# Mamba blocks of a four-layer megakernel: X for one pair of images, deeper rings with sums one group later, output projection and fusion in one accumulation, statistics by ScalarE, and the last sum of softplus moved

## The chip, the cores and the metric

The kernel runs on one core of one Trainium2 chip, in float32 throughout. The metric is the device time of one launch in microseconds (us). Before the change it is 9826.69 us, the median of 3 runs (9817.78 to 9828.18).

## The reference, cut to what matters

Four layers follow one another on an image tensor x of 4 x 96 x 64 x 64. Layers 0 and 2 are the Mamba block below (the only code that the change touches); layer 1 is another state-space block and layer 3 a ConvNeXt block. In layers 0 and 2:

```python
# seq: (b, L=4096, 96), two sublayers i; DIN=192, DSTATE=16, DTRANK=6
seq = seq + _mamba_block(seq, ...)          # for i in range(2)
#   h = layernorm(seq); xs, z = split(h @ in_w)
#   xc = silu(causal 4-tap conv of xs)
#   dt, Bm, Cm = split(xc @ xproj_w)
#   delta = softplus(dt @ dt_w + dt_b);  dA = exp(delta * A)
#   hstates = scan over L of  s = dA * s + delta * Bm * xc
#   y = (hstates . Cm + Dp * xc) * silu(z);  return y @ out_w
gp = relu(x.mean((2, 3)) @ gp_w.T + gp_b)   # global branch, from the input
out = fus_w @ concat([mamba_out, gp broadcast]) + fus_b
out = (out - mean(out)) * rsqrt(var(out) + EPS) * bn_g + bn_b   # over batch and pixels
return out + residual
```

## The kernel before, in words

The four images go in two pairs. One step of `Scan.run` (L383) is one pair, one sublayer (`sub`) and one chunk of T = 512 positions, so a Mamba stage has 2 x 2 x 8 = 32 steps, and the launch has two such stages. Channels of both images of a pair (2 x 192) fill three 128-row tiles j.

**Front.** `mamba_front` (L155) makes what a step needs: layernorm (PE, ScalarE, VectorE, GpSimd), convolution and projections on PE into the two PSUM banks "mm", SiLU, then delta by `softplus` (L260) and `du = delta * xz`. The 128 x 512 tiles delta and du go to DRAM (`dd`, `dg`, L251), from where the scan reads them with a broadcast over the 16 states. It is a generator: the scan loop takes one or two pieces of the next step's front per group (`PACE`, L256), so front and scan of neighbouring steps run together.

**Groups.** A step has 24 groups (j, q, half), each two scans of 128 x 512. Group n passes these stages at these lags (L395 on): `load` (L288, lag -4: SyncE, called SP, issues the broadcast DMAs into a ring "da" of 6 tiles), `decay` and `spread` (-2 and -1: ScalarE takes exp of delta times A; PE spreads du into the PSUM ring "bs", L313, or, in one group of four, du arrives by DMA and GpSimd multiplies it by B, L308), `scan` (0: VectorE multiplies by B, L335, and runs two scans into `hs`, L340; GpSimd multiplies by C into `hc`, L342), `sums` (+2: PE sums hc over the states into `py`, L361). `hs` and `hc` have 3 buffers each. After the last group of a j, `close` (+3, L369) multiplies py by silu(z) on VectorE, `project` (+4, L377) is the output projection on PE into `po`, with VectorE adding it to X (L381), and `fuse` (+5, sublayer 1 only) multiplies X by the fusion weights (L510), adds the bias on ScalarE (L511), takes `bn_stats` on VectorE (L512) and stores the chunk (L513). [...]The order within a queue follows the program only roughly: the tile framework's scheduler moves single instructions past one another, so lines that neighbour in the code need not neighbour in the trace.

**X.** The residual stream of all four images stays in SBUF, 4 x 4096 floats in each of 96 partitions. It is loaded once (L473, L525), and VectorE sums each image over its 4096 positions (L532) for the global branch.

Of the kernel before, what the change touches and what calls it, by code (L numbers as in the profile page):

```python
# [18 lines left out]
F32 = mybir.dt.float32  # L19
AF = mybir.ActivationFunctionType  # L20
# [134 lines left out]
def mamba_front(tc, k, X, pools, wt, pair, c, h, made):  # L155
# [14 lines left out]
    for b in range(2):  # L170
        pc = bank("pc")[:C]
        nc.tensor.matmul(
            pc, lhsT=k.center, rhs=X[:, 2 * pair + b, ds(c * T, T)], start=True, stop=True
        )
        sq = work.tile([P, T], F32, tag="ua", name="sq")[:C]
        nc.scalar.activation(sq, pc, AF.Square)
        yield
        pv = bank("pv")[:C]
        nc.tensor.matmul(pv, lhsT=k.mean, rhs=sq, start=True, stop=True)
        rs = work.tile([P, T], F32, tag="lg", name="rs")[:C]  # L180
        rsqrt(k.act, rs, pv, k.eps[:C])
        yield
        dst = h[:C, b, 3 : 3 + T]
        nc.vector.tensor_tensor(dst, pc, rs, ALU.mult)
        nc.gpsimd.tensor_scalar(dst, dst, wt["ln"][:, 0:1], wt["ln"][:, 1:2], ALU.mult, ALU.add)
# [45 lines left out]
    for j in range(3):  # L231
        pt = bank("pt")
        for r0, r1, d0, d1, b in SEGS[j]:
            half = ds(HALFP * b, HALFP)
            nc.tensor.matmul(
                pt[r0:r1], lhsT=wt["dt"][half, d0:d1], rhs=dbl[half], start=True, stop=True,
            )
        delta = work.tile([P, T], F32, name="delta", bufs=2)
        softplus(nc, k.act, work, delta, pt)
        yield  # L240
        if j == 0:
            for b in range(2):
                for q in range(2):
                    r = HALFP * b + (QUART if q else RANK + 1)
                    nc.sync.dma_start(
                        bc[:, b, q], rows[r : r + NST, None].to_broadcast([NST, HEIGHT, T])
                    )
        nc.gpsimd.tensor_tensor(du[:, j], delta, xz[:, j], ALU.mult)
        for name, x in (("dd", delta), ("dg", du[:, j])):
            made[name, j] = dram.tile([P, T], F32, name=f"{name}{j}")  # L250
            nc.sync.dma_start(made[name, j], x)  # L251
# [8 lines left out]
def softplus(nc, act, work, out, x):  # L260

    u = work.tile([P, T], F32, tag="ua", name="ua")
    t = work.tile([P, T], F32, tag="lg", name="lg")
    nc.scalar.activation(u, x, AF.Abs)
# [5 lines left out]
    nc.vector.scalar_tensor_tensor(t, x, 1.0, u, ALU.subtract, ALU.subtract, reverse1=True)  # L270
    nc.gpsimd.tensor_tensor(out, out, t, ALU.add)


class Scan:
# [8 lines left out]

    def __init__(self, tc, k, X, pools, sel, carry, fuse):
        self.tc, self.k, self.X, self.sel, self.carry, self.fuse = tc, k, X, sel, carry, fuse
        self.state, self.psum = pools

    def load(self, g):  # L288

        for name, which in (("da", "dd"), ("du", "dg")) if g["dma"] else (("da", "dd"),):  # L290
            g[name] = self.state.tile([P, GS, T], F32, tag="da", name=name, bufs=6)
            for i in range(GS):
# [37 lines left out]
    def scan(self, g):  # L330
# [3 lines left out]
        if not g["dma"]:  # L334
            nc.vector.tensor_tensor(dbx, dbx, self.b_or_c(g, 0), ALU.mult)  # L335
        hs = self.state.tile([P, GS, T], F32, name="hs", bufs=3)
        for i in range(GS):
            n = NQU * g["quarters"][i] + g["q"]
            init = 0.0 if c == 0 else self.carry[:, j, n : n + 1]
            nc.vector.tensor_tensor_scan(hs[:, i], da[:, i], dbx[:, i], init, ALU.mult, ALU.add)  # L340
        g["hc"] = self.state.tile([P, GS, T], F32, name="hc", bufs=3)
        nc.gpsimd.tensor_tensor(g["hc"], hs, self.b_or_c(g, 1), ALU.mult)  # L342
# [28 lines left out]
    def project(self, g, b):  # L371

        nc = self.tc.nc
        xz, wt = g["made"]["xz"], g["wt"]
        po = self.psum.tile([P, T], F32, tag="po", name="po", bufs=1)[:C]
        for n, (j, r0, r1) in enumerate(ROWS[b]):
            nc.tensor.matmul(  # L377
                po, lhsT=wt["out"][r0:r1, j], rhs=xz[r0:r1, j], start=(n == 0), stop=(n == 1)
            )
        xs = self.X[:, 2 * g["pair"] + b, ds(g["c"] * T, T)]  # L380
        nc.vector.tensor_tensor(xs, xs, po, ALU.add)  # L381

    def run(self, steps, wts, front, first):  # L383
# [12 lines left out]
        ahead = iter(())  # L396
        for n in range(-4, total + 6):
            slot = (n + LEAD) % each
# [8 lines left out]

            if (g := at(3)) and g["last"]:
                self.close(g)
            for stage, lag in (  # L410
                (self.load, -4), (self.spread, -1), (self.decay, -2), (self.scan, 0), (self.sums, 2),
            ):
                if g := at(lag):
                    stage(g)

            for lag, what in ((4, self.project), (5, self.fuse)):
                if (g := at(lag)) and g["last"] and g["j"] and (g["sub"] or lag == 4):
                    what(g, g["j"] - 1)
# [48 lines left out]
def mamba_fusion(ctx: ExitStack, tc, k, src, dst, w):  # L467

    nc = tc.nc
    one = ctx.enter_context(tc.tile_pool(name="m1", bufs=1))  # L470
    X = one.tile([C, B, L], F32, name="X")
    for b in range(2):
# [27 lines left out]
    for q in range(NQU):  # L500
        pq = psum.tile([P, T], F32, tag="mm", name="pq")[:, :QUART]
        nc.tensor.transpose(pq, sel["du"][:QUART, 0, q], k.ident[:QUART, :QUART])
        nc.vector.tensor_copy(sel["sum"][:, q], pq)
    stats = one.tile([C, B * NT, nc.vector.BN_STATS_DIM], F32, name="stats")

    def fuse(g, b):
        b, c = 2 * g["pair"] + b, g["c"]
        xs = X[:, b, ds(c * T, T)]
        pf = psum.tile([P, T], F32, tag="po", name="pf", bufs=1)[:C]
        nc.tensor.matmul(pf, lhsT=fus[:, 0], rhs=xs, start=True, stop=True)  # L510
        nc.scalar.activation(xs, pf, AF.Identity, bias=gb[:, b : b + 1])  # L511
        nc.vector.bn_stats(stats[:, b * NT + c], xs)  # L512
        nc.sync.dma_start(dst[b, :, ds(c * T, T)], xs)  # L513

# [7 lines left out]

    for b in range(B):
        rest = slice(T if b < 2 else 0, L)
        nc.sync.dma_start(X[:, b, rest], src[b, :, rest])  # L525

    gsum = one.tile([C, B], F32, name="gsum")
    made = {}
    for n, _ in enumerate(front(0, made)):
        if n % 4 == 3 and n // 4 - 1 in range(B):  # L530
            b = n // 4 - 1
            nc.vector.reduce_sum(gsum[:, b : b + 1], X[:, b], axis=AX.X)  # L532
    wts.append(mamba_weights(nc, k.act, k.ident, one, w, 1, one7))

# [4 lines left out]
    vec = one.tile([C, 4], F32, name="vec")  # L539
    nc.sync.dma_start(vec, w["vecs"])  # L540


# [8 lines left out]

    Scan(tc, k, X, (state, psum), sel, carry, fuse).run(steps, wts, front, made)

    norm = k.norms.pop()
    mv = one.tile([C, 2], F32, name="mv")
    nc.vector.bn_aggr(mv, stats)
    sc, sh = norm[:, 0:1], norm[:, 1:2]
    rsqrt(k.act, sc, mv[:, 1:2], k.eps[:C])
    nc.vector.tensor_tensor(sc, sc, vec[:, 2:3], ALU.mult)
    nc.vector.tensor_tensor(sh, mv[:, 0:1], sc, ALU.mult)  # L560
    nc.vector.tensor_tensor(sh, vec[:, 3:4], sh, ALU.subtract)
# [848 lines left out]
```

## Time and profile before

| what | value |
|---|---|
| median of 3 runs | 9826.69 us |
| the profiled execution, its own time | 9824.4 us |
| its span (first to last instruction) | 9822.7 us |
| first Mamba stage (layer 0) | 0 to 3062 us |
| layer 1 | 3062 to about 6176 us |
| second Mamba stage (layer 2) | about 6176 to 9237 us |
| layer 3 | 9237 to 9822.7 us |
| mean granted TensorE clock over the span | 0.939 |

How it is read: a row of a group gives busy time and the mean of one instruction, and after the bar the idle time of the engine ahead of these instructions with what ended it ("<-"). A row by stretch gives, for a window of time, each engine's busy time and number of instructions, then the granted clock, the mean share of the 16 DMA engines and the bandwidth. PEld is weight loading, SPq the queue of SyncE that issues DMAs. Most questions are put to the window from 200 to 2900 us, in which steps of the first stage follow one another. It holds 88 instructions of L369, three to a step, so 29.33 steps of 92.05 us.

### The profile page before, as it was taken

How to read it: one execution, taken by the hardware profiler on the slowest of the kernel's cores; microseconds unless marked ns; L12 is line 12 of the kernel's file. 1: busy time of each engine (PE TensorE's matmuls, PEld its weight loads, DVE VectorE, ACT ScalarE, POOL GpSimd, SP SyncE). 2: the span in 40 equal slices, each digit the busy share in tenths (PEclk: the TensorE clock that was granted, in tenths of full speed). 3: DMA queues.
4: the chain of work that ended last, by engine and by line, in shares of the span. 5: the costliest groups of instructions: out<-in, count | busy, mean ns of one | idle time of the engine just before them, and what ended most of it. 6: DMA issues, size and time to landing. Idle time of an engine off the chain costs nothing. (4 is left out here: it accounts for less than half of the span.)

```text
span 9822.7 us, 110113 instructions
## 1 busy us (share of the span) xinstructions
PE 8432.2 (86%) x32750; PEld 3481.8 (35%) x32750; DVE 8131.3 (83%) x11036; ACT 5529.8 (56%) x10516; POOL 6879.9 (70%) x4573
## 2 busy tenths in 40 slices
PE   7888888888886998998998889788888888888678
PEld 1222212222222776776776767212212122222122
DVE  7999999999995666666666667699999999999787
ACT  5566566666663455555445555466666666666345
POOL 6888888888884555555555555588888888888511
PEclk8999999999997999999999999899999999999789
DMA  7677777777774222222222321576777777777653
GB/s 184 199 206 205 201 209 203 205 207 200 205 204 134 69 73 81 82 67 83 81 67 77 86 69 60 156 203 201 207 207 201 209 202 201 207 204 201 163 120 83
DMA packets 810274, 1528.80 MB, mean 156 GB/s; under 512 B 126381, under 2 KB 131913, under 8 KB 805834
## 3 DMA queue, kind: packets, MB, share of 16 engines
q1 hardware_dynamic: 809674, 1521.76, 55.1%
q8 instruction: 260, 4.26, 0.2%
q14 instruction: 340, 2.79, 0.1%
HBM read 1224.56 MB, written 150.08 MB: 140 GB/s over the span
## 5 line engine op out<-in xcount | busy, mean ns | idle before, releaser
L342 POOL TENSOR_TENSOR hc<-hs,bc 128x1024 f32<-128x1024 f32 x1536 | 3610.4, 2357 | 626.5 <-DVE hs L340 560.6
L340 DVE TENSOR_TENSOR_SCAN hs<-da,carry,bs 128x512 f32<-128x512 f32 x2016 | 2467.0, 1265 | 81.1 <-DVE bs L335 2.3
L107 ACT ACTIVATE da<-da,w_a 128x512 f32<-128x512 f32 x2304 | 1616.3, 716 | 1265.9 <-DMA da<-dd 1220.7
L361 PE MATMUL py<-hc,selsum 128*32 128x512 f32 x6144 | 1795.7, 636 | 466.4 <-POOL hc L342 453.2
L313 PE MATMUL bs<-du,seldu 64*128 64x512 f32 x4608 | 1572.6, 676 | 211.1 <-DVE hs L340 199.2
L335 DVE TENSOR_TENSOR bs<-bs,bc 128x1024 f32<-128x1024 f32 x1152 | 1398.3, 1214 | 181.6 <-PE bs L313 178.4
L308 POOL TENSOR_TENSOR du<-du,bc 128x1024 f32<-128x1024 f32 x384 | 905.5, 2358 | 272.5 <-DMA du<-dg 149.3
L361 PEld LDWEIGHTS py<-hc,selsum 128*32 128x32 f32 x6144 | 239.9, 110 | 1810.2 <-POOL hc L342 1124.8
L879 POOL TENSOR_TENSOR seg<-seg,cb 128x384 f32<-128x384 f32 x512 | 515.3, 1008 | 513.9 <-DVE cb L878 429.7
L313 PEld LDWEIGHTS bs<-du,seldu 64*128 64x128 f32 x4608 | 446.2, 195 | 1205.4 <-DVE hs L340 857.5
L863 DVE TENSOR_SCALAR seg<-dr,dac 128x128 f32<-128x128 f32 x1536 | 646.7, 455 | 271.5 <-PE y L908 264.2
L194 PE MATMUL pu<-h,w_conv 96*128 96x512 f32 (+3 forms) x2048 | 835.6, 628 | 8.8 <-ACT rs L107 8.7
L340 DVE TENSOR_TENSOR_SCAN hs<-bs,carry,du 128x512 f32<-128x512 f32 x672 | 823.6, 1260 | 7.5 <-issue 3.8
L814 PE MATMUL front<-pk,sconv 128*128 128x512 f32 x1536 | 756.4, 610 | 30.1 <-ACT z L802 24.8
L918 POOL TENSOR_TENSOR y<-y,xs 128x192 f32<-128x192 f32 x496 | 295.4, 595 | 626.2 <-DVE y L917 619.4
L931 ACT ACTIVATE y<-yz 128x192 f32<-128x192 f32 x512 | 186.1, 363 | 910.7 <-DVE yz L930 909.8
L883 POOL TENSOR_TENSOR xs<-pre,coef 128x576 f32<-128x576 f32 x512 | 598.8, 1174 | 64.6 <-ACT pre L112 32.3
L825 PE MATMUL front<-sconv,pk 128*128 128x192 f32 x3072 | 573.9, 330 | 51.5 <-DVE pre L830 46.2
L345 ACT COPY carry<-hs 128x2 f32<-128x2 f32 x1344 | 250.8, 187 | 571.0 <-DVE hs L340 567.3
L825 PEld LDWEIGHTS front<-sconv,pk 128*128 128x128 f32 x3072 | 497.5, 190 | 82.3 <-DVE pre L830 72.6
L107 ACT ACTIVATE bs<-da,w_a 128x512 f32<-128x512 f32 x768 | 522.0, 680 | 3.7 <-DMA da<-dd 1.5
L908 PEld LDWEIGHTS y<-xs,seg 128*128 128x128 f32 x3072 | 439.9, 205 | 142.4 <-issue 79.6
(200 smaller groups left out, 13612.7 us busy)
## 6 DMA issues: line engine op xcount, KB each, us to landing
da<-dd SPq DMA_DIRECT2D x3072, 256.0 KB
du<-dg SPq DMA_DIRECT2D x768, 256.0 KB
dr<-rows SPq DMA_DIRECT2D x256, 384.0 KB
bc<-rows SPq DMA_DIRECT2D x256, 256.0 KB
dd<-delta SPq DMA_DIRECT2D x192, 256.0 KB
dg<-du SPq DMA_DIRECT2D x192, 256.0 KB
pk<-xn SPq DMA_DIRECT2D x128, 384.0 KB
pk<-xn SPq DMA_DIRECT2D x128, 256.0 KB
```

The lines of the kernel that those rows point to most:

```text
L107: self.last = self.scalar.activation(out, in_, func, **kw)
L194: nc.tensor.matmul(pu[r0:r1], lhsT=wt["conv"][:kk, tap, d0:d1], rhs=h[:kk, b, ds(tap, T)], start=(tap == 0), stop=(tap == 3),)
L308: nc.gpsimd.tensor_tensor(g["du"], g["du"], self.b_or_c(g, 0), ALU.mult)
L313: nc.tensor.matmul(g["bs"][:, i], lhsT=self.sel["du"][rows, g["half"], g["q"]], rhs=g["made"]["du"][rows, g["j"]], start=True, stop=True,)
L335: nc.vector.tensor_tensor(dbx, dbx, self.b_or_c(g, 0), ALU.mult)
L340: nc.vector.tensor_tensor_scan(hs[:, i], da[:, i], dbx[:, i], init, ALU.mult, ALU.add)
L342: nc.gpsimd.tensor_tensor(g["hc"], hs, self.b_or_c(g, 1), ALU.mult)
L361: nc.tensor.matmul(py[rows], lhsT=self.sel["sum"][:, g["q"]], rhs=g["hc"][:, i], start=(g["q"] == 0), stop=(g["q"] == NQU - 1),)
L814: nc.tensor.matmul(p, lhsT=self.conv[:, i, DI + q * DST : DI + (q + 1) * DST], rhs=pk[:, i, ds(c * T, T)], start=(i == 0), stop=(i == 2),)
L825: nc.tensor.matmul(p, lhsT=pk[:, i, ds(c * Q, Q)], rhs=self.conv[:, i, :DI], start=(i == 0), stop=(i == 2),)
L863: nc.vector.tensor_scalar(seg[:, h], g["pair"]["dr"][:, c % 2 * NH + h], made["dac"][:, n0 + h : n0 + h + 1], 0.0, ALU.subtract, ALU.min,)
L883: nc.gpsimd.tensor_tensor(xs, x.to_broadcast([P, 3, NH, HD]), coef.to_broadcast([P, 3, NH, HD]), ALU.mult)
```

## The change

What it does: X holds one pair (the second pair's chunks are loaded over the first pair's as these are stored, and the sums of images 2 and 3 are taken from pieces that pass through the "da" ring at the start). The ring "da" has 8 tiles and loads at lag -5; `hs` and `hc` have 4 buffers; `sums`, `close`, `project` come one group later. `project` accumulates X through the identity (sublayer 0) or the fusion weights (sublayer 1) and the projected y in one PSUM group; for sublayer 1 the output weights are multiplied by the fusion weights at the start. ScalarE writes X back. The batch statistics come from accumulator outputs of ScalarE. The last addition of `softplus` moves next to the multiplication that follows it, and its scratch tile "lg" has two buffers.

```diff
@@ mamba_front
-            pc, lhsT=k.center, rhs=X[:, 2 * pair + b, ds(c * T, T)], start=True, stop=True
+            pc, lhsT=k.center, rhs=X[:, b, ds(c * T, T)], start=True, stop=True
...
-        softplus(nc, k.act, work, delta, pt)
+        lost = softplus(nc, k.act, work, delta, pt)
         yield
...
+        nc.gpsimd.tensor_tensor(delta, delta, lost, ALU.add)
         nc.gpsimd.tensor_tensor(du[:, j], delta, xz[:, j], ALU.mult)
@@ softplus
-    t = work.tile([P, T], F32, tag="lg", name="lg")
+    t = work.tile([P, T], F32, tag="lg", name="lg", bufs=2)
...
-    nc.gpsimd.tensor_tensor(out, out, t, ALU.add)
+    return t
@@ Scan.load
-            g[name] = self.state.tile([P, GS, T], F32, tag="da", name=name, bufs=6)
+            g[name] = self.state.tile([P, GS, T], F32, tag="da", name=name, bufs=8)
@@ Scan.scan
-        hs = self.state.tile([P, GS, T], F32, name="hs", bufs=3)
+        hs = self.state.tile([P, GS, T], F32, name="hs", bufs=4)
...
-        g["hc"] = self.state.tile([P, GS, T], F32, name="hc", bufs=3)
+        g["hc"] = self.state.tile([P, GS, T], F32, name="hc", bufs=4)
@@ Scan.project
+        xs = self.X[:, b, ds(g["c"] * T, T)]
+        nc.tensor.matmul(po, lhsT=wt["of_x"], rhs=xs, start=True, stop=False)
         for n, (j, r0, r1) in enumerate(ROWS[b]):
             nc.tensor.matmul(
-                po, lhsT=wt["out"][r0:r1, j], rhs=xz[r0:r1, j], start=(n == 0), stop=(n == 1)
-            )
-        xs = self.X[:, 2 * g["pair"] + b, ds(g["c"] * T, T)]
-        nc.vector.tensor_tensor(xs, xs, po, ALU.add)
+                po, lhsT=wt["out"][r0:r1, j], rhs=xz[r0:r1, j], start=False, stop=(n == 1)
+            )
+        if g["sub"] == 0:
+            nc.scalar.copy(xs, po)
+        else:
+            self.fuse(g, b, xs, po)
@@ Scan.run
-            if (g := at(3)) and g["last"]:
+            if (g := at(4)) and g["last"]:
                 self.close(g)
...
-                (self.load, -4), (self.spread, -1), (self.decay, -2), (self.scan, 0), (self.sums, 2),
+                (self.load, -5), (self.spread, -1), (self.decay, -2), (self.scan, 0), (self.sums, 3),
...
-            for lag, what in ((4, self.project), (5, self.fuse)):
+            for lag, what in ((5, self.project), (6, self.spread_out)):
@@ mamba_fusion
-    X = one.tile([C, B, L], F32, name="X")
+    X = one.tile([C, 2, L], F32, name="X")
...
-    def fuse(g, b):
-        b, c = 2 * g["pair"] + b, g["c"]
-        xs = X[:, b, ds(c * T, T)]
-        pf = psum.tile([P, T], F32, tag="po", name="pf", bufs=1)[:C]
-        nc.tensor.matmul(pf, lhsT=fus[:, 0], rhs=xs, start=True, stop=True)
-        nc.scalar.activation(xs, pf, AF.Identity, bias=gb[:, b : b + 1])
-        nc.vector.bn_stats(stats[:, b * NT + c], xs)
-        nc.sync.dma_start(dst[b, :, ds(c * T, T)], xs)
+    def fuse(g, b, xs, po):
+        n = (2 * g["pair"] + b) * NT + g["c"]
+        nc.scalar.activation(
+            xs, po, AF.Identity, bias=gb[:, n // NT : n // NT + 1], accum_out=sums[:, n : n + 1]
+        )
+        nc.sync.dma_start(dst[n // NT, :, ds(g["c"] * T, T)], xs)
+
+    def spread_out(g, b):
+        n = (2 * g["pair"] + b) * NT + g["c"]
+        xs = X[:, b, ds(g["c"] * T, T)]
+        nc.scalar.mul(means[:, n : n + 1], sums[:, n : n + 1], -1.0 / T)
+        sq = work.tile([P, T], F32, tag="ua", name="sqs")[:C]
+        nc.scalar.activation(
+            sq, xs, AF.Square, bias=means[:, n : n + 1], accum_out=squares[:, n : n + 1]
+        )
+        if g["pair"] == 0:
+            nc.sync.dma_start(xs, src[2 + b, :, ds(g["c"] * T, T)])
...
-            nc.vector.reduce_sum(gsum[:, b : b + 1], X[:, b], axis=AX.X)
+            nc.vector.reduce_sum(gsum[:, b : b + 1], X[:, b], axis=AX.X)
+        if n in (13, 15, 17, 19):
+            for m in range(n - 13, n - 11):
+                b, c = 2 + m // (L // BLK), m % (L // BLK)
+                x = state.tile([P, GS, T], F32, tag="da", name="x", bufs=8)[:C]
...
+                nc.vector.reduce_sum(parts[:, b, c : c + 1], x.rearrange("c i t -> c (i t)"), axis=AX.X)
+    nc.vector.reduce_sum(gsum[:, 2:], parts[:, 2:], axis=AX.X)
...
+    wts[0]["of_x"], wts[1]["of_x"] = k.ident[:C, :C], fus[:, 0]
+    for j in range(3):
+        pt = psum.tile([P, T], F32, tag="mm", name="pt")[:C, :P]
+        nc.tensor.transpose(pt, wts[1]["out"][:, j], k.ident)
+        turned = work.tile([P, T], F32, tag="ua", name="turned")[:C, :P]
+        nc.scalar.copy(turned, pt)
+        pw = psum.tile([P, T], F32, tag="mm", name="pw")[:, :C]
+        nc.tensor.matmul(pw, lhsT=turned, rhs=fus[:, 0], start=True, stop=True)
+        nc.scalar.copy(wts[1]["out"][:, j], pw)
```

After the scans, the one `bn_aggr` gives way to three reductions over 32 columns and four operations on columns of 1 or 32 elements on VectorE, and the same two table functions on ScalarE.

## The prediction

> **What bounds the kernel now.** I read the busy totals of the page first, then the stretch in the middle of the first Mamba stage, then VectorE's groups there, and last the waits of each engine in that stretch.
>
> ```profile
> PE 8432.2 (86%) x32750; PEld 3481.8 (35%) x32750; DVE 8131.3 (83%) x11036; ACT 5529.8 (56%) x10516; POOL 6879.9 (70%) x4573
> ...
> DVE  7999999999995666666666667699999999999787
> ```
>
> The totals mix four layers: PE leads. By slices, VectorE (DVE) stands at 9 through both Mamba stages and at 6 between them. The change touches only these stages, so the stretch decides:
>
> ```profile
> 200.00:2900.00 2700.00, 2362.65 (x7236) 549.73 (x7234) 2525.68 (x2336) 1676.42 (x3011) 2309.64 (x1109) 0.96 0.72 204
> ```
>
> After the window come busy times of PE, weight load, DVE, ScalarE (ACT) and GpSimd (POOL). The second stage (6350 to 9050) has 2530.67 of 2700 for DVE, so what holds for one holds for both. With 29.33 steps in the window, a step is 92.05 us: DVE 86.1, PE 80.6, POOL 78.7, ACT 57.2. DVE is nearest to full, with 174.3 us of idle time in the window, 5.94 a step. Its groups tell where that lies:
>
> ```profile
> L340 DVE TENSOR_TENSOR_SCAN hs<-da,carry,bs 128x512 f32<-128x512 f32 x944 | 1155.2, 1265 | 37.9 <-ACT da L107 1.0 <-POOL du L308 1.0 <-DVE bs L335 0.5
> L335 DVE TENSOR_TENSOR bs<-bs,bc 128x1024 f32<-128x1024 f32 x525 | 637.2, 1214 | 80.5 <-PE bs L313 79.1
> ...
> L270 DVE SCALAR_TENSOR_TENSOR lg<-pt,ua 128x512 f32<-128x512 f32 x87 | 59.2, 681 | 18.2 <-ACT pt L268 16.8 <-POOL du L308 0.6
> ...
> L381 DVE TENSOR_TENSOR X<-X,po 96x512 f32<-96x512 f32 x58 | 38.7, 668 | 11.4 <-PE bs L313 8.9 <-PE po L377 2.5
> L512 DVE BATCH_NORM_STATS2 stats<-X 96x6 f32<-96x512 f32 x28 | 18.8, 671 | 0.3 <-ACT X L511 0.3
> ```
>
> The scans hardly wait for data; the largest wait, 80.5 us, is for PE's spread of du, and L381 and L512 are the two groups that the change takes off DVE. Why PE is late, though it idles 12.5%, its own waits and those of ACT and SP say:
>
> ```profile
> PE py L361 <- POOL hc L342: 187.1, 234, 4.5
> PE bs L313 <- DVE hs L340: 85.4, 132, 1.6
> PE pc L172 <- DVE lg L270: 41.4, 26, 3.4
> ```
>
> ```profile
> ACT da L107 <- DMA da<-dd: 538.2, 334, 5.8
> ```
>
> ```profile
> SPq L295 <- DVE hs L340: 921.6, 497, 6.0
> SPq L251 <- POOL delta L271: 217.9, 87, 4.4
> SPq L245 <- DMA rows<-dbl: 101.7, 29, 4.9
> SPq L251 <- POOL du L248: 81.8, 87, 1.0
> ```
>
> (Waited in all, times, longest.) PE stands 187 us at the state sums for hc of two groups back; the next bs lies behind that in its queue, and DVE needs the bs. It is a ring: scan, hc, sums, bs, scan. ACT waits 538 us for decay loads, and SP waits 922 us for a free "da" tile before it can issue them: the loads start late because the ring is short.
>
> **What the Trainium skill says.** (1) "GPSIMD Engine Reference", Specifications: POOL's SBUF interface is shared with VectorE, with contention when a VectorE instruction has two SBUF inputs. L381 reads X from SBUF and po from PSUM, so taking it away should not speed POOL up; no run here shows contention, and the hc multiplication stays at its mean of 2357 ns. (2) "TensorE: Matmul & The Clock Gate", What's actually happening: the clock is throttled by default and activity releases it. The trace agrees in direction: 0.96 granted in the window, with PE 87% busy, and 0.82 from 2958 to 3048 us, where it is 71% busy. A denser PE thus should not lose clock. (3) "DMA: Bandwidth & Descriptors", Two DMAs through the same engine are not ordered: the issuing engine has to wait for the first DMA's semaphore. That makes the new load of X behind its store a wait on SP. The trace has the same pattern: bc after rows costs SP 101.7/29 = 3.5 us each.
>
> **The change part by part**, all from the profiled execution (9824.4 us; the median of the runs is 2.3 higher).
>
> VectorE's work. L381 and L512 go: 57.5 us in the window. DVE instructions overlap in the records (rows sum to 2619 us, busy is 2526, 2336 instructions: 0.040 us each), so their 86 instructions are worth 57.5 - 3.4 = 54.1 us, or **1.84 us a step**, all on the bounding engine. The wait of 11.4 us ahead of L381 goes too: 0.39 a step.
>
> Sums one group later, hs and hc of 4, ring of 8. The sums get one more group (92.05/24 = 3.8 us) of slack against waits of at most 4.5 us on POOL, so most of PE's 187 us should go and with it a good part of the 80.5 us of DVE. I cannot read the share off the trace: bounds are none and all (0 to 2.74 a step); I take half, **1.37**. What remains is PE's own load (next part) and the bs ring, still 2 deep. The loads start one group earlier; ACT waits less and its front work (L268 and the layernorm) comes earlier. DVE's waits for those (L270 18.2, L267 4.2, L184 12.6, together 35 us or 1.19 a step) I let fall by a third, **0.40** (bounds 0 and 1.19). The 46.7 us ahead of scans (1.59 a step) are short gaps that no cause is named for; they stay.
>
> PE. of_x adds two matmuls a step; pf (L510) takes away two in half of the steps. A matmul of 512 columns in float32 is two instructions, and takes some 1.05 us where PE runs dense (pc rows follow one another with bs and py at that distance). Net +2.1 - 1.05 = 1.05 us: PE 81.6 a step. It is beside DVE's work as long as PE stays under the step; if that cover goes, it costs the 1.05.
>
> ACT. Sublayer 0: two copies from PSUM like L209's, 0.58 each. Sublayer 1: the Identity stays (0.674) with an accumulator output added, whose read stands in layer 1's trace as 187 ns (L931); the small multiplication is like L345 (0.186), the Square like L176 (0.588) with another 0.187. So +1.16 or +2.30, mean 1.73: ACT 58.9 of 88, hidden. Square and Identity run in the exp/ln table set in the trace (L176, no load ahead), so no table load comes with them. The copy is queued in the same group as the carry copy (L345), which waits for the scan anyway; behind it lie the next exps, two groups ahead of need.
>
> Softplus's last sum. POOL does the same instruction (1269 ns), later. POOL waited 0.5 us in all for it, so nothing is gained there; "lg" of two buffers ends ACT's 14 us of waits for L271. But the dd store in SP's queue waits for that sum: 217.9/87 = 2.5 us now, up to one hc (2.36 us) more; three a step is 7.1 us on SP, and behind it stand da loads. Cover: SP idles 921.6/29.33 = 31 us a step for ring tiles, and the loads are one group (3.8 us) further ahead. I take 0; uncovered it is 7.1.
>
> X of one pair. In 8 of 32 steps SP waits for two stores to land before the reload, at the 3.5 us of L245: 7 us, same cover; 0 (bounds 0 and 112 us in both stages). 3 MB more per stage at 204 GB/s is 15 us of DMA time at a share of 0.72: hidden.
>
> Start of a stage. Pieces of images 2 and 3 replace whole images: same bytes, same DVE elements, before the first scan at 76.6 us. New is the product of fusion and output weights: three times transpose, copy, matmul, copy, dependent, 0.45 + 0.25 + 0.45 + 0.25 with hops about 1.7 us: +5 us a stage (0 to 6), estimated from the small matmul L544 (0.46) and the small ACT instructions L546 and L550 (0.26).
>
> Last step of a stage. It has no front beside it, and DVE stands at `close` for py: 5.00, 3.42 and 3.42 us. One group later these become about 1.3, 0 and 0: -10.5, with the removed work -12.3 a stage. At the very end the chain loses the X add, pf, bn_stats and bn_aggr (0.68 + 2.02 + 0.69 + 1.02 = 4.4) and gains two accumulator reads, the scaling, the Square and six more short DVE operations of 0.19 (0.19 + 0.19 + 0.19 + 0.59 + 1.14 = 2.3): -2.
>
> Sum: 1.84 + 0.40 (the 11.4 and 0.3 us of waits) + 1.37 + 0.40 = 4.01 us a step; 62 steps: -249; last steps -25, ends -4, starts +10: **-268 us**, so 9824.4 - 268 = 9556, and 9558 on the scale of the median. A step then is 88.0 us: DVE 84.3, PE 81.6, POOL 78.7. What is late next is PE's bs still.
>
> **The rivals.**
> All waits but the gaps ahead of the scans go: 1.84 + 4.35 = 6.19 a step, -384 - 19 = -403: 9421. For it: every such wait traces back to one of the loosened rings. Against: PE would have to run at 81.6 of 85.9, 95%.
> No wait goes: the longer lag only shifts PE's wait from hc to bs. DVE's work alone, 1.84 with L381's wait taken over by others: -114 - 19 = -133: 9691. For it: the bs ring keeps two banks and PE waits 85 us for hs already.
> SP becomes the bound, and the kernel is **slower**: the dd stores hold SP behind POOL, da loads behind them come late, ACT and the scans starve. If the 7.1 us a step is exposed whole and the deeper rings return nothing: 7.1 - 1.84 - 0.40 = +4.9 a step, +302 - 19: about 10107. It turns slower from the point where more than some 4.3 us a step (4.01 and the 19 us of the ends) is exposed, were the other gains as forecast. Against: SP's 31 us of idle and the third of a step's groups that lie between stores and use.
> PE takes it all: 81.6 busy and the present waits other than hc, with its weight loads, fill the 92: no change, about 9820.
>
> **How the numbers follow.** Forecast 0.58; all waits 0.12; work alone 0.17; SP 0.10; PE 0.03. Faster by over 0.2% (20 us, about what a measurement of this kernel can tell from no change): 0.58 + 0.12 + 0.17 = 0.87; within 0.03; slower 0.10. The range runs from the all-waits case, 9415, to past the work-alone case with half of the reload's 112 us, 9735; SP, PE and the tails outside, about 0.18, are left out.
>
> **What would show it.** Right: DVE busy near 95 to 96% in mid-stage; its wait for bs near 40 us in a window of this length; PE's wait for hc under 60; no L381 or L512 groups; ACT's wait for da loads well down; no py waits at the last step's closes. Wrong: the bs wait unchanged with PE now waiting for DVE's hs (work alone), scans waiting for ACT da with SP waiting at the dd stores (SP), or a granted clock much under 0.96.

## The result and the profile after

The changed kernel takes 9928.55 us (median of 4 runs, 9906.36 to 9936.89) against 9827.44 us (4 runs) of the kernel before on the same chip: ratio 1.0099, 95% interval 1.0085 to 1.0113. It is 1% slower, where 9558 was forecast. The profiled execution's span is 9920.5 us, 97.8 more than before, and the mean clock 0.934 (before 0.939).

The busy totals of the page, and VectorE's slices, answer to the first view of before:

```profile
PE 8591.2 (87%) x32896; PEld 3517.4 (35%) x32896; DVE 8039.3 (81%) x10870; ACT 5599.9 (56%) x10798; POOL 6861.3 (69%) x4573
...
DVE  7988898998995666666666667688999889999887
```

VectorE lost work, 92 us in all, but its slices in the Mamba stages went from 9 to 8 and 9: it got less busy, not faster. The stretch of mid-stage, columns as before:

```profile
200.00:2900.00 2700.00, 2392.72 (x7182) 552.01 (x7180) 2438.11 (x2213) 1682.87 (x3081) 2262.72 (x1089) 0.95 0.76 201
```

The window holds 86 instructions of L371 (the old L369), 28.67 steps of 94.2 us. VectorE is busy for 85.0 us a step (86.1 before), idle for 9.1 (5.94 before). The second stage's window has 2424.99 us of VectorE, so it is the same there. Measured by the first multiplication of each step in the window, a step grew from 92.42 to 94.14 us. From the first multiplication of a stage's first step to that of its last step, the two stages together take 5897.7 us, 5784.7 before: 113.0 more, so the steps carry more than the whole loss of 97.8, and the ends gave some 15 us back. VectorE's groups in the window:

```profile
L337 DVE TENSOR_TENSOR bs<-bs,bc 128x1024 f32<-128x1024 f32 x517 | 627.3, 1213 | 159.0 <-PE bs L315 158.7
...
L271 DVE SCALAR_TENSOR_TENSOR lg<-pt,ua 128x512 f32<-128x512 f32 x86 | 57.7, 671 | 0.0
...
L184 DVE TENSOR_TENSOR h<-pc,rs 96x512 f32<-96x512 f32 x56 | 38.4, 686 | 49.2 <-ACT rs L107 48.8
```

The groups of the X addition and of the batch statistics are gone and the wait ahead of softplus's L271 too. But the wait for PE's spread, 80.5 us before, is 159.0, and the one for the layernorm (L184) went from 12.6 to 49.2. By group of a step, the wait for the spread stayed where it was and a new one came: groups 10 to 23 have 71.3 us of it (69.4 before), groups 0 to 9 have 87.4 (9.7 before), nearly all at groups 0 and 2, the start of a step.

The waits of PE, ScalarE and SP in the same window (waited in all, times, longest):

```profile
ACT da L107 <- DMA da<-dd: 251.9, 323, 3.7
PE py L363 <- POOL hc L344: 166.5, 125, 4.3
...
PE bs L315 <- DVE hs L342: 84.6, 113, 2.0
...
ACT sqs L526 <- PE pv L179: 33.5, 12, 4.4
PE pv L179 <- ACT sq L176: 31.7, 12, 3.0
```

```profile
SPq L297 <- DVE hs L342: 795.6, 416, 13.0
SPq L252 <- POOL delta L248: 300.6, 86, 6.4
```

The deeper ring did its part for the loads: ScalarE's wait for them halved, from 538.2. The later sums did not: PE waits for hc nearly as long as before (187.1). New is that ScalarE's statistics (L526, "sqs") stand 33.5 us for PE, and PE's layernorm 31.7 for ScalarE. The statistics need nothing that pv makes; they write the scratch tile "ua", which pv is still reading. SP's wait at the delta store grew, but SP still has 796 us of waiting for free tiles. One step's start in the timeline shows how the new waits chain, ScalarE and the last reader of its scratch first:

```profile
2146.54 0.66 DVE L271 SCALAR_TENSOR_TENSOR lg<-pt,ua 128x512 f32<-128x512 f32 x1
...
2149.02 0.72 ACT L107 ACTIVATE da<-da,w_a 128x512 f32<-128x512 f32 x1 [2.17 <-DMA da<-dd]
2149.65 0.57 ACT L176 ACTIVATE sq<-pc 96x512 f32<-96x512 f32 x1
```

```profile
2150.27 1.42 PE L179 MATMUL pv<-sq,mean 96*96 96x512 f32 x2 [2.47 <-ACT sq L176]
...
2153.47 2.07 PE L315 MATMUL bs<-du,seldu 64*128 64x512 f32 x2
...
2157.43 2.07 PE L315 MATMUL bs<-du,seldu 64*128 64x512 f32 x2
```

```profile
2159.54 1.23 DVE L337 TENSOR_TENSOR bs<-bs,bc 128x1024 f32<-128x1024 f32 x1 [2.99 <-PE bs L315]
```

The layernorm's Square writes the scratch "ua", which softplus reads until 2147.20 (L271); from then on it waits in ScalarE's queue behind an exp whose load is late. PE stands at pv, with the spreads behind it in its queue. The granted clock is at half from 2150.9 (the pairs of matmuls take 2.07 us; at 2144.72 a pair took 1.10), and VectorE, two spreads later, waits 2.99 us. This step is one of sublayer 0, in which ScalarE takes no statistics.

### The profile page after: what moved, and what is told of

The parts are those of the page before. It is cut to its first block, busy times and chain, and to the rows that moved or that the text cites. A ratio compares the mean times of both kernels' runs of the same rounds, so it can differ in the third digit from the quotient of the medians.

```text
span 9920.5 us, 109872 instructions
## 1 busy us (share of the span) xinstructions
PE 8591.2 (87%) x32896; PEld 3517.4 (35%) x32896; DVE 8039.3 (81%) x10870; ACT 5599.9 (56%) x10798; POOL 6861.3 (69%) x4573
## 5 line engine op out<-in xcount | busy, mean ns | idle before, releaser
L363 PE MATMUL py<-hc,selsum 128*32 128x512 f32 x6144 | 1767.6, 635 | 429.4 <-POOL hc L344 397.1
L315 PE MATMUL bs<-du,seldu 64*128 64x512 f32 x4608 | 1516.7, 666 | 216.2 <-DVE hs L342 201.5
L315 PEld LDWEIGHTS bs<-du,seldu 64*128 64x128 f32 x4608 | 422.2, 192 | 1260.3 <-DVE hs L342 832.3
L194 PE MATMUL pu<-h,w_conv 96*128 96x512 f32 (+3 forms) x2048 | 856.7, 639 | 2.8 <-ACT rs L107 2.8
```

Of the source, the lines that this page charges most:

```text
L194: nc.tensor.matmul(pu[r0:r1], lhsT=wt["conv"][:kk, tap, d0:d1], rhs=h[:kk, b, ds(tap, T)], start=(tap == 0), stop=(tap == 3),)
L315: nc.tensor.matmul(g["bs"][:, i], lhsT=self.sel["du"][rows, g["half"], g["q"]], rhs=g["made"]["du"][rows, g["j"]], start=True, stop=True,)
L363: nc.tensor.matmul(py[rows], lhsT=self.sel["sum"][:, g["q"]], rhs=g["hc"][:, i], start=(g["q"] == 0), stop=(g["q"] == NQU - 1),)
```

## The experiments

Three theories stood against one another after the result. **Order**: the queue in which PE meets spreads and sums decides, and neither the lag nor VectorE's relief can act through it. **Replacement**: ScalarE's new work stands in the way, not by its amount but by what waits behind it. **Amount**: PE has too much to do, or runs at half clock. The expectations on record call them by letters: A is SP held up behind softplus's later sum, B is the merge (of projection, addition to X and statistics), C and later O the order, D is PE's work and clock as the bound, V is VectorE as the bound with PE having time to spare. Ratios are to the kernel before on the same chip, with the 95% interval.

First comes PE's queue as the traces have it. For each group of a step, this is how many groups the newest spread ahead of its sums in PE's queue is ahead of it (mean over the steps, without the last of each stage; the code asks for 3 before and 4 after, and one group in four has no spread, so 3/2 and 4/3 alternate):

```
group   0 1 2 3 4 5 6 7 8 9 | 10 11  12 13 14 15 16  17 18 19 20  21  22 23
before  3 3 2 3 3 3 2 3 3 3 | 2  1   2  3  2  1  2   3  2  1  2   2.5 2  1.3
after   4 3 4 4 4 3 4 4 4 3 | 2  1.3 2  3  2  1  2.7 3  2  1  2.9 2.4 2  2.2
```

The later lag exists only in the first ten groups of a step. In the rest, where VectorE waited most before (69.4 of 79.1 us), the tile framework's scheduler put the sums nearly where they had been. That is why the old wait did not go. It is not why a new one came: that one stands at groups 0 and 2, where the later lag is there.

**Parts undone in the changed kernel.** e1 puts softplus's last addition back:

```diff
+        nc.gpsimd.tensor_tensor(delta, delta, lost, ALU.add)   # in front, after softplus
-        nc.gpsimd.tensor_tensor(delta, delta, lost, ALU.add)   # beside the multiplication
```

> Edit: the changed kernel (9928 us) with softplus's last sum back where it was, one piece of the front earlier; the scratch tile keeps two buffers. Theory A (the dd stores hold SP behind POOL's later sum, the da loads behind them come late, ACT's layernorm work and then PE start late and PE's clock drops): most of the 100 us lost come back and more, 9700 to 9850. Theory B (the merged projection costs PE more than it saves DVE): no change, 9910 to 9945. Theory C (later sums and deeper rings change the order of the queues for the worse): no change either.

9937.44 us, 1.0103 (1.0083 to 1.0123): no difference, and PE's sums stand as in the changed kernel. SP's wait at the delta store stays too (300.7 us in the window), so that wait did not come from the moved addition.

e2 takes the merge back: projection and fusion apart, X added and statistics taken by VectorE; X of one pair, deep rings and later sums stay.

```diff
-        nc.tensor.matmul(po, lhsT=wt["of_x"], rhs=xs, start=True, stop=False)
+        nc.vector.tensor_tensor(xs, xs, po, ALU.add)
...
+        nc.vector.bn_stats(stats[:, n], xs)
```

> Edit: the changed kernel with projection and fusion apart again, X added by VectorE, bn_stats and bn_aggr on VectorE; X of one pair, deep rings, later sums and the later softplus sum stay. Theory B (the merge is what costs: PE's extra matmul a step, ACT's copies and squares queued ahead of the layernorm): at or under the kernel before, 9750 to 9830. Theories A and C: VectorE gets 1.8 us a step back to do, so 9930 to 10050.

9888.69 us, 1.0053 (1.0035 to 1.0071): 40 us faster than the changed kernel, with VectorE's work back, and between the two forecasts. So the merge costs more than it saves. VectorE's wait for the spread is 15.1 us at groups 0 to 9 and 105.0 at the others: without the merge the new wait at the start of a step is gone, and a smaller one stands at group 22 (39.5 us).

e3 takes all rings and lags back, e4 only the lags of sums, close and project.

```diff
-                (self.load, -5), (self.spread, -1), (self.decay, -2), (self.scan, 0), (self.sums, 3),
+                (self.load, -5), (self.spread, -1), (self.decay, -2), (self.scan, 0), (self.sums, 2),
```

> Edit: the changed kernel with rings of 6, 3 and 3 and all lags as before (loads -4, sums 2, close 3, project 4, spread_out 5). Theory C (later sums or earlier loads reorder the queues for the worse): 9750 to 9850. Theory A: slower still, since the longer ring is what covers the held SP, 9950 to 10050. Theory B: about as the changed kernel, 9900 to 9960.

> Edit: the changed kernel with the deep rings and loads at -5, but sums, close and project one group earlier, as before. Theory C by the lags: as e3, 9750 to 9850. If C is true by the loads at -5 instead, this stays at 9900 to 9950 while e3 is fast. Theories A and B: 9910 to 9960.

e3: 10054.16 us, 1.0224 (1.0202 to 1.0247). e4: 10102.61 us, 1.0271 (1.0254 to 1.0289). Without the rings and lags the changed kernel is slower still, by more than any of the theories had forecast; VectorE's wait for the spread in e3 is 190.4 us. But in e3 the queue order also moved (at group 16 the newest spread is 0.45 groups ahead, not 2.7), so these two runs do not give the price of the rings by themselves. The rings alone in the kernel before weren't tried.

**Amount.** e5 adds one matmul ahead of each projection to the kernel before (its sum is overwritten), e7 leaves `of_x` out of the changed kernel, e8 adds four idle matmuls a step at the layernorm.

```diff
# e5
+        nc.tensor.matmul(po, lhsT=self.k.ident[:C, :C], rhs=xs, start=True, stop=True)
# e7
-        nc.tensor.matmul(po, lhsT=wt["of_x"], rhs=xs, start=True, stop=False)
# e8
+        for _ in range(2):
+            nc.tensor.matmul(pv, lhsT=k.mean, rhs=X[:, b, ds(c * T, T)], start=True, stop=True)
```

> Edit: the kernel before (9827 us) with one more matmul ahead of each output projection (X through the identity into po, overwritten by the projection), two a step, and nothing else. Theory D (PE is the co-bound: around the step boundary it runs at half clock and can't keep up, so PE work added there goes straight into the time): 1 to 2 us a step, 9890 to 9960. Theory V (VectorE binds, PE has 12% to spare): 9820 to 9840.

> Edit: the changed kernel without the matmul that brings X into the projection's sum; the residual is left out of the computation. Theory D: two matmuls a step less on PE, 1 to 2 us a step, 9790 to 9860. Theory V: no change, 9910 to 9940.

> Edit: the changed kernel with two idle matmuls per image into the layernorm's second bank (overwritten afterwards), in the stretch at the step boundary where PE runs at half clock; four a step. If the half clock there is what makes PE late (theory D), the granted clock rises over 0.95 and the time falls to 9700 to 9880 in spite of 4 us more PE work a step. If PE's amount of work alone counts, 10050 to 10250 at an unchanged clock. Theory V: 9920 to 9950.

e5: 9992.93 us, 1.016 (1.014 to 1.0181). e7: 9988.27 us, 1.0145 (1.0114 to 1.0176), at a clock of 0.910. e8: 10020.19 us, 1.0178 (1.015 to 1.0206), at 0.941. More work on PE, less, and more with a higher clock are all slower, each outside what D and V forecast. e5 alone spoke for the amount, but like e3 it has the order moved (0.45 at group 16), and in e7 and e8 it moved as well (2.2 at group 17 for 3; 3.0 to 3.9 at groups 20 to 23). The pinned runs below decide.

**VectorE's relief.** e6 takes the X addition and the statistics from the kernel before (both left out of the computation, nothing in their place).

```diff
-        nc.vector.tensor_tensor(xs, xs, po, ALU.add)
...
-        nc.vector.bn_stats(stats[:, b * NT + c], xs)
```

> Edit: the kernel before without VectorE's addition to X and without bn_stats; the residual sum and the batch statistics are left out of the computation. Theory V: 1.84 to 2.2 us a step less, 9685 to 9710. Theory D: VectorE's time comes back as waits for PE's spread, 9770 to 9830.

9830.32 us, 0.9996 (0.9986 to 1.0006): removing 57.5 us of the busiest engine's work in the window gives nothing. Where it went, the waits of e6 show:

```profile
DVE bs L335 <- PE bs L313: 131.9, 106, 7.3
```

79.1 us before, 131.9 now, and PE's sums stand nearly where they stood in the kernel before: most of the time VectorE saves it waits for PE.

e9 makes X one pair in the kernel before and changes nothing else.

```diff
+    X = one.tile([C, 2, L], F32, name="X")
...
+        if g["pair"] == 0:
+            nc.sync.dma_start(xs, src[2 + of, :, ds(c * T, T)])
```

> Edit: the kernel before with X of one pair alone (reloads behind the stores, sums of images 2 and 3 from pieces); rings, lags, projection and statistics as before. Its PE queue has the same order in a step as the kernel before. If the smaller X costs by itself (later starts, SP held at the reloads, slower packets), 9880 to 10000; if not, 9820 to 9850.

9880.11 us, 1.0035 (1.0022 to 1.0049), with the matmuls of a step in the same order: X of one pair costs some 34 us. The mean busy share of the DMA engines in the window rises from 0.72 to 0.77 at the same bandwidth (203 GB/s, before 204).

**The order pinned.** The next kernels say in the code where the sums stand: each matmul of L361 is ordered behind the newest spread (an ordering within PE's own queue; no semaphore). The newest spread is then 3/2 (before) or 4/3 (after) groups ahead everywhere.

```diff
-            nc.tensor.matmul(
+            self.spreads = nc.tensor.matmul(      # in spread
...
+            if self.spreads is not None:          # in sums
+                self.k.act._behind(ins, self.spreads)
```

e10 is the changed kernel pinned, e11 the kernel before, e12 is e2 pinned.

> Edit: the changed kernel with the sums' matmuls pinned behind the newest spread in PE's queue, as the program writes them (an order only, no wait). In the changed kernel's queue the sums stand 3 to 4 groups behind the spread in the first ten groups of a step and 1 to 3 behind it in the others, which is where VectorE waits. Theory O (the scheduler's order takes the extra group of slack away where it is needed): VectorE's wait for the spread falls by half and the time to 9650 to 9850. Theory D (PE's work at the clock it gets is the bound, whatever the order): 9900 to 9950.

> Edit: the same pinned order in the kernel before, where the sums then stand 2 to 3 groups behind. Theory O: some of the 2.7 us a step of waits for the spread go, 9700 to 9800. Theory D: 9815 to 9850.

> Edit: the pinned order in the kernel of the second experiment (projection, addition to X and statistics as before; X of one pair, deep rings, later sums). Under theory O the merge of the projection should then be a gain or nothing: this one at or above the pinned changed kernel. If the merge costs by its PE work (theory D), this one lies 40 us or more under the pinned changed kernel and under 9800.

e10: 9880.11 us, 1.0052 (1.0032 to 1.0072). e11: 9852.11 us, 1.0009 (1.0003 to 1.0016). e12: 9848.58 us, 1.0005 (0.9994 to 1.0017). Pinning does nothing for the kernel before, though VectorE's wait for the spread drops to 24.3 us there (a wait for softplus, 80.1 us, takes its place), but half of the changed kernel's loss goes. Neither theory had forecast e10 or e12: both fell between O and D. With e2, four kernels make a square:

| above the kernel before | order of the scheduler | order pinned |
|---|---|---|
| changed kernel | +0.99% | +0.52% (e10) |
| merge taken back | +0.53% (e2) | +0.05% (e12) |

Order and merge cost about 0.47% each, and they add; with the intervals of the runs, each is known to some 0.25 points. What is left in the pinned, merged kernel e10 is this:

```profile
PE pv L179 <- ACT sq L176: 100.1, 29, 5.7
...
DVE bs L338 <- PE bs L316: 94.5, 68, 4.1
```

In e12 the first line has 18.4 us. e10's longest such wait, in the timeline:

```profile
1576.71 0.68 DVE L271 SCALAR_TENSOR_TENSOR lg<-pt,ua 128x512 f32<-128x512 f32 x1
...
1582.24 0.72 ACT L107 ACTIVATE da<-da,w_a 128x512 f32<-128x512 f32 x1 [7.12 <-DMA da<-dd]
1582.87 0.58 ACT L176 ACTIVATE sq<-pc 96x512 f32<-96x512 f32 x1
```

Its input was ready at 1570, and softplus last read the scratch that it writes until 1577.39. For the 5.5 us from there on it waited for an exp that has nothing to do with it, and that exp for its load.

e13 and e14 ask for the amount again, with the order held: two matmuls a step more, three less (e14 leaves the D term out of the computation). e15 takes VectorE's two operations out as e6 did, e16 both those and the D term (all left out).

```diff
# e13
+        nc.tensor.matmul(po, lhsT=self.k.ident[:C, :C], rhs=xs, start=True, stop=True)
# e14, e16
-            nc.tensor.matmul(
-                py, lhsT=g["wt"]["d"][:, g["j"]], rhs=g["made"]["xz"][:, g["j"]], start=False,
-                stop=False,
-            )
# e15, e16
-        nc.vector.tensor_tensor(xs, xs, po, ALU.add)
...
-        nc.vector.bn_stats(stats[:, b * NT + c], xs)
```

> Edit: the kernel before with the pinned order (9852 us) and one more matmul ahead of each output projection, two a step, overwritten by it. PE as the bound: 2 to 2.5 us a step, 9970 to 10020. VectorE as the bound or PE with slack: 9840 to 9870.

> Edit: the kernel before with the pinned order and without the matmul that adds D times x to the sums (left out of the computation), three a step, some 3 us of PE. PE as the bound: 9650 to 9720. If PE only gives back what it gains by running longer at half clock: 9820 to 9860 at a lower granted clock. VectorE as the bound: 9840 to 9870.

> Edit: the kernel before with the pinned order, without VectorE's addition to X and without bn_stats (residual and statistics left out of the computation). VectorE as the bound: 9690 to 9740. PE as the bound: 9830 to 9860.

> Edit: the two omissions of the runs before together. PE as the bound: as the run without the D matmuls. Co-bound: clearly below both, 9550 to 9680. If the half clock takes all slack: 9800 to 9850.

e13: 9855.94 us, 1.0029 (1.0021 to 1.0036). e14: 9858.58 us, 1.0028 (1.002 to 1.0035). Five matmuls a step of difference change nothing, so PE's amount of work is not what binds here. The edit that cost 1.6% in e5 costs 0.2% against e11 once the order is held. (e13 and e14 both lie 0.2% above e11, the one with more work on PE and the one with less; no run tells why.) e15: 9736.38 us, 0.9904 (0.9889 to 0.9919). e16: 9741.69 us, 0.9908 (0.9893 to 0.9922). The edit that gave nothing in e6 gives 1% once the order is held. e16 gives no more than e15, which none of its three forecasts had. VectorE's wait for the spread in e15:

```profile
DVE bs L336 <- PE bs L314: 37.9, 53, 3.3
```

**The replacement.** e17 is e11 with the merge alone: `of_x`, ScalarE's write of X and ScalarE's statistics (X of four images, rings, lags and softplus as before). e18 is e17 with one word changed, a scratch of its own for the statistics' Square; in e17 and in the change it shares the scratch "ua" with the layernorm's Square and with softplus.

```diff
-        sq = work.tile([P, T], F32, tag="ua", name="sqs")[:C]
+        sq = work.tile([P, T], F32, name="sqs")[:C]
```

> Edit: the kernel before with the pinned order (9852 us) and only the merge: X through PE into the projection, ScalarE writes X back, statistics by ScalarE's accumulators; X of four images, rings, lags and softplus as before. If the replacement is hidden beside VectorE, as the run without VectorE's two instructions: 9720 to 9770, and the loss lies in the other parts. If the replacement takes the gain (ScalarE waits for PE's projection ahead of the layernorm and the softplus, PE stands for them): 9840 to 9960, with PE waiting for the layernorm's Square or VectorE for softplus.

> e17's kernel with a scratch tile of its own for ScalarE's Square with accumulator; in e17 that Square writes the scratch which softplus's chain uses too, so it waits for softplus's last reader on VectorE (1.6 us in a sublayer of the first kind, up to 4.7 us a wait), with the whole of ScalarE's queue behind it. The step of the first half layer in e17 is as long as with the work left out (92.8 against 92.7 us), that of the second 95.1 against 91.0. If the shared scratch is what costs: a step of the second kind near 92, time 9740 to 9790 us. If it is ScalarE's added instructions themselves (2 means, 2 Squares, their accumulator reads, the copy, in an in-order queue), wherever the scratch lies: 9820 to 9850 us as in e17, and VectorE's waits for the spread stay near 120 us a window. In between, about 9790 to 9820: both.

e17: 9839.6 us, 1.0005 (0.9997 to 1.0014): the replacement takes back all that e15 gave. e18: 9795.21 us, 0.9946 (0.9926 to 0.9967), the fastest complete kernel of the study, faster than e17 and than the kernel before; it lies in the range that was forecast for both causes together. By half layer, measured by the first multiplication of each step (without the start and end of a stage and the first step of each half layer; one execution of each kernel), a step takes, in us:

| kernel | sublayer 0: first, second stage | sublayer 1: first, second stage |
|---|---|---|
| before | 91.9, 92.1 | 93.4, 93.4 |
| changed | 95.6, 96.2 | 94.4, 94.1 |
| e2, merge taken back | 92.7, 93.0 | 93.9, 94.8 |
| e10, changed, pinned | 93.5, 93.9 | 95.6, 96.1 |
| e12, merge back, pinned | 91.3, 92.1 | 95.5, 96.5 |
| e11, before, pinned | 93.7, 93.3 | 93.3, 93.4 |
| e15, work left out | 92.7, 92.2 | 91.0, 91.1 |
| e17, merge alone | 92.8, 93.7 | 95.1, 94.4 |
| e18, scratch of its own | 92.8, 93.1 | 92.1, 92.4 |

In e17 most of what the replacement takes back lies in sublayer 1, where the statistics are: 4.1 and 3.3 us a step over e15, of which 3.0 and 2.0 go with the scratch (over e11, which has VectorE's work, e17 is 1.8 and 1.0 us longer there). In sublayer 0, where ScalarE only copies X, it is free in the first stage and costs 1.5 us in the second. In the changed kernel it is the other way round: the merge (changed against e2, e10 against e12) costs 1.8 to 3.2 us a step in sublayer 0, which has no statistics, and at most 0.5 in sublayer 1. So what e18 mends is not what the merge costs in the changed kernel. Some waits of e17 and then e18:

```profile
DVE bs L337 <- PE bs L315: 119.7, 84, 3.7
...
ACT rs L107 <- PE pv L179: 53.5, 29, 4.2
ACT sq L176 <- DVE lg L270: 25.7, 12, 4.6
...
ACT sqs L528 <- DVE lg L270: 21.0, 13, 4.7
```

```profile
DVE bs L337 <- PE bs L315: 83.4, 62, 4.5
...
ACT sq L176 <- DVE lg L270: 46.6, 25, 5.1
ACT rs L107 <- PE pv L179: 33.7, 26, 3.0
```

The 21.0 us at "sqs" are the direct wait for the last reader of the scratch. That wait did not go: in e18 it stands at the layernorm's Square ("sq"), which still shares the scratch with softplus, and the two together are 46.7 us in e17 and 46.6 in e18. What fell is the waiting of ScalarE for pv and of VectorE for the spreads. The one word also moved instructions: 916 of the 10786 places in ScalarE's queue hold another instruction in e18, and 268 of the 32896 in PE's. In e17, 28 of the 64 Squares of the statistics stand directly ahead of a layernorm's Square; in e18 none does, nor in the changed kernel. So the gain belongs to the scratch together with the order that was built for it; the two were not separated.

## Why the prediction was wrong

**"86 instructions are worth 54.1 us, or 1.84 us a step, all on the bounding engine": wrong where it was used, right by size.** e15 gives about 0.0105 of 9845 between it and e11, 103 us or 1.7 us a step. But e6 gives 0. The prediction read VectorE as bound because it was the busiest, though it also read that its idle time was a wait for PE behind PE's sums. As long as that order stands, less work on VectorE only makes it wait longer (e6).

**"The sums get one more group of slack, so most of PE's 187 us should go and with it a good part of the 80.5 us; I take half": failed.** The wait for hc stayed at 166.5 and that for the spread doubled. The lag in the code is not the lag in the queue: in groups 10 to 23 the scheduler left the sums nearly where they were, and there the wait stayed (71.3 us after 69.4). The rest of the doubling came at groups 0 and 2; there it goes when the merge is taken back (e2), so it belongs to the next term. The text on the kernel before says that the order follows the program only roughly; the sum took the code's order as the queue's all the same. With the order pinned, the changed kernel gains 0.47%, still not the 1.37 us a step that were forecast.

**"ACT +1.73 a step, hidden", with the next exps behind it, two groups ahead of need: failed.** The amount was close (ScalarE's busy time a step went from 57.2 to 58.7 us; the Square with bias and accumulator took 721 ns instead of the 588 taken from a Square without bias). The cover failed: the page "PSUM — Partial Sum Buffer" of the Trainium skill, Engine vs sequencer instructions, says that ScalarE's queue is strictly first in, first out, and the traces agree (e10: a Square with input and scratch free started 5.5 us later, behind an exp). Behind the next exps lies the next step's layernorm, then PE's pv, then the spreads, and that path the prediction did not follow. The seven steps of sublayer 0 from 1683 to 2354 us in the changed kernel, and the same steps in e2 (1674 to 2324 us), show it:

```profile
PE pv L179 <- ACT sq L176: 16.1, 6, 3.0
DVE h L184 <- ACT rs L107: 21.3, 13, 5.9
```

```profile
DVE h L184 <- ACT rs L107: 0.3, 1, 0.3
```

In e2 PE has no wait of 0.15 us or more at pv there. The stretch is 21 us longer with the merge, about what VectorE waits more for the layernorm. What makes the layernorm late was not tested: in sublayer 0 the merge takes VectorE's addition away, adds ScalarE's copy of X and PE's `of_x`, and changes the order that the scheduler builds around them.

It also wasn't asked which buffer the new Square writes. In e18 against e17 that, with the order that comes with it, is 0.59%. The remaining 0.42% between e18 and e15 is ScalarE's and PE's added work with its place in the queues; these were not separated. Nor is it shown why the merge costs 0.47% in the changed kernel but 0.04% less than nothing in e17 against e11; e10's 100 us at pv, against 9.4 us in e17, says where to look. The changed kernel with a scratch of its own wasn't run; by the half layers it should bring little, since its merge costs hardly anything where the statistics are.

**X of one pair at 0: too low.** e9 measures 0.35%, about 34 us, within the bounds of 0 and 112. The reload, the pieces at the start and the busier DMA engines weren't told apart.

**A third of the waits for the front: failed in sum.** L270's wait went as argued; the layernorm's, which is a wait for ScalarE, grew from 12.6 to 49.2.

**Right:** the loads come earlier; softplus's later addition is worth 0 (e1), and with it the rival of SP as the bound falls for the change as it is; PE's added work in itself is nearly hidden in the pinned kernel before (e13, e14). All ends together gave some 15 us of the 19. The first scan starts at 81.3 us, 76.6 before, close to the 5 us taken, but by luck: the product of weights that these stood for is in e17 and e18 too, and there it starts at 77.4 and 76.9.

The rival in which no wait goes came nearest: VectorE still waits for the spread. But the shift of PE's wait from hc to bs that it named did not come (166.5 and 84.6 us, 187.1 and 85.4 before), and it too left VectorE's 1.84 standing. The rival that was slower named SP's queue, with ScalarE starved of loads; ScalarE's wait for loads halved instead. On the clock, the prediction drew from "TensorE: Matmul & The Clock Gate" (What's actually happening) that a denser PE should not lose any. PE became denser (2392.72 us busy for 2362.65) and the window went from 0.96 to 0.95, the second stage's to 0.94. That is no cause by itself: e12 ran at 0.919 and took as long as the kernel before.

How the 1% comes together: the square shows that 0.47% goes when the merge is taken back, in either order, and 0.47% when the order is pinned, with the merge or without. With the order pinned, the rest, X of one pair with rings and lags, is about 0 (e12 against e11). In the scheduler's order the same rest costs 0.53% (e2), and X of one pair alone already 0.35% (e9), though the scheduler's order costs the kernel before nothing (e11). So the half that is called order here may as well be the price of the smaller X in that order; X of one pair with the order pinned wasn't run. By which instruction the merge costs its half is open as well.

## What to carry to other kernels

Before counting work removed from the busiest engine as time, ask which queue feeds it and in what order: read the order that was built, not the lags in the code, and where the order matters, pin it. When work moves to an idle engine, its amount is the smaller question; look up which buffers the moved instructions write and who else holds them, and what stands behind them in that engine's queue. Test a relief and its replacement apart: leaving the work out (e15) and putting it elsewhere (e17, e18) took three runs to show the gain and what ate it. And before carrying a finding from one kernel to another, look where in the step and in which half of the work each of them loses its time: here e17 and the changed kernel lose it in different sublayers.

## What the runs showed of the hardware

In these runs neither the granted clock nor the time went with how much PE has to do. Taking `of_x` out of the changed kernel lowered the clock from 0.934 to 0.910 and made it slower; e8's idle matmuls raised it to 0.941, slower too (in both the order of PE's queue moved as well); e12 fell to 0.919 at no cost. The clock records of the changed kernel's trace hold two values, 1.0 and 0.5. The pair of float32 matmuls of 512 columns at L379 took 1.10 us at 2144.72, where 1.0 was granted, and the pair at L172 took 2.02 at 2141.48, where 0.5 was.

X of one pair raised the mean busy share of the DMA engines from 0.72 to 0.77 over the whole window (e9) at the same bandwidth, though 3 MB more in a stage are under 1% of its traffic. e17, with X of four images and the merge, shows 0.76 as well, e15 0.73. No run here settles why.

An accumulator output of ScalarE cost an instruction of its own here, 191 ns after the Identity (L516) and 187 after the Square (L526) in the changed kernel, as the prediction took from layer 1.
